# Norm rows and transposed copies of a self-attention layer on ScalarE in place of VectorE

## The chip, the cores and the metric

The kernel runs on one core of a Trainium2 chip. The metric is the device time of one execution in microseconds. The core has five engines that each work through their own instructions in order and wait for each other by semaphores: TensorE (PE in the profile, with its weight loads as PEld), VectorE (DVE), ScalarE (ACT), GpSimd (POOL) and SyncE (SP), which here only issues transfers.

## The reference

Two decoder layers over 32 sequences of 100 tokens with 256 features. Each layer adds self-attention, cross-attention and a mixture of experts to `x`, each applied to the layer norm of `x`:

```python
x = x + _L0_attn_ref(_layernorm(x, axis=-1), ...)
x = x + _L0_xattn_ref(_layernorm(x, axis=-1), ctx_512, ...)
x = x + _L0_ffn_ref(_layernorm(x, axis=-1), ...)
x = x + _L1_attn_ref(_layernorm(x, axis=-1), L1_attn_W1, L1_attn_b1, L1_attn_W2, L1_attn_b2)
x = x + _L1_xattn_ref(_layernorm(x, axis=-1), ctx_512, ...)
x = x + _L1_ffn_ref(_layernorm(x, axis=-1), ...)
```

The layer norm has no learned scale or shift. Layer 1's self-attention has no softmax: the masked scores multiply the values directly.

```python
def _layernorm(x, axis=-1, eps=1e-05):
    m = jnp.mean(x, axis=axis, keepdims=True)
    v = jnp.var(x, axis=axis, keepdims=True)
    return (x - m) / jnp.sqrt(v + eps)

def _L1_attn_ref(x, W1, b1, W2, b2):
    bs, t, d = x.shape
    h = 16
    kqv = x @ W1 + b1
    k, q, v = jnp.split(kqv, 3, axis=-1)
    ...
    mask = jnp.tril(jnp.ones((t, t), dtype=bool))
    attn = jnp.where(mask, jnp.einsum('bhqd,bhkd->bhqk', q, k), 0.0)
    out = jnp.einsum('bhqk,bhkd->bhqd', attn, v)
    out = out.transpose(0, 2, 1, 3).reshape(bs, t, d)
    return out @ W2 + b2
```

## The kernel before

The 3200 tokens lie in SBUF as `x`, 25 tiles of 128 tokens with 256 features. A sequence has 100 tokens, so tiles and sequences don't line up; `parts` and `pieces` say which rows of a tile belong to which sequence. The six parts of the reference run one after the other, each as a loop over sequences, with the norms of the next part made inside the loop of the one before. Everything is float32.

Layer 1's self-attention is `l1_attn`. Before its loop the first tiles are prepared (the fill); then one step per sequence `b` follows. A group is three tiles (the first has four) and serves four sequences. What happens to a tile `f` on its way:

- *Load.* `gather0` (L1356) has SyncE load two rows of layer 0's expert results per token (`yk`, six buffers; the transfer at L1361), and VectorE adds them, weighted, to `x` in two operations (L1368). From the third group on, a load is also tied to an earlier tile's values (`behind`).
- *Stats.* `norm_stats`: mean and variance on VectorE (L219, L222); once a group is complete, one addition (L224), a square root on ScalarE (L225) and a reciprocal on VectorE (L228).
- *Norm row.* `norm_rows` makes `xn` = (x - mean) * rstd, one VectorE operation per tile (L231). Afterwards GpSimd adds the output bias `bo` to `x` (L246).
- *Transposes.* `norm_turn` has TensorE transpose `xn` into a PSUM bank (L253), and `evac` copies the bank to `xnT`. `evac` counts its calls and gives every second to ScalarE (L172), the others to VectorE (L173).
- *Projections.* `proj` makes queries and keys of four sequences (TensorE, L178); ScalarE moves them out with the bias (L1035, L1038). `vals` makes a tile's values; VectorE adds the bias into `vt` (L1048, two operations), and SyncE moves the rows from `vt` to the sequences' `v` (L1055).

In step `b`: the 32 score matmuls (`scores`), into four banks that VectorE empties with the causal mask (L1072, four operations); one projection of the next group; `vals` of a tile in 24 of the steps; `out` of sequence `b - 2` where that completes a tile (L283 adds it to `x`, followed by that tile's stats for the next part); in the first three steps of four, load and stats of a tile of the group after the next; in the fourth, `turn`, that is norm rows and transposes of the next group; and the 32 matmuls of the values of sequence `b - 1` (L1082), copied by ScalarE to `zT` (L1089). `next_norm` prepares norm rows for layer 1's cross-attention on GpSimd (`xnx`); their transposes come a step later, through the same `norm_turn`.

The eight PSUM banks are handed out in turn, so a matmul block also waits for the copy out of what used its bank eight allocations before. TensorE's order is as written (`manual_schedule`). The order on the other engines is chosen by the framework's scheduler from the dependencies. One of these is set by hand: the gather additions come behind `self.last_row`, the norm row that was made last:

```python
self.gather0(pool, fs[i], self.last_row, made[-6] if len(made) > 5 else None)
```

Of the kernel before, what the change touches and what calls it, by code (L numbers as in the profile page):

```python
# [9 lines left out]
F32 = mybir.dt.float32  # L10
I32 = mybir.dt.int32
U32 = mybir.dt.uint32
AF = mybir.ActivationFunctionType
ALU = mybir.AluOpType
AX = mybir.AxisListType

P = 128
# [104 lines left out]
class Kernel:  # L122
# [84 lines left out]
    def norm_stats(self, f, groups, after=None):  # L207
# [15 lines left out]
        if i == n - 1:  # L223
# [3 lines left out]
                self.depend(got, [self.norm_after.ins], "behind the fill's copies")  # L227
            nc.vector.reciprocal(rstd, rstd)  # L228

    def norm_row(self, f, out, eng):  # L230
        return eng.tensor_scalar(out, self.x[:, f, :], *self.norms[f], ALU.subtract, ALU.mult)  # L231

    def norm_rows(self, f, n, bias=None, rows=None, after=None, eng=None):

        nc = self.nc
        if rows is not None:
            xn = rows[:, f : f + n, :]
        else:
            xn = self.lnp.tile([P, 2, XROW], F32, tag="xn", name="xn")[:, :n, :D]
        for j in range(n):  # L240
            got = self.last_row = self.norm_row(f + j, xn[:, j, :], eng or nc.vector)
            if after is not None:
                self.depend(got, [after.ins], "behind the work of its step")
        if bias is not None:
            for j in range(n):
                nc.gpsimd.tensor_tensor(self.x[:, f + j, :], self.x[:, f + j, :], bias, ALU.add)  # L246
        return xn

    def norm_turn(self, f, n, xn, bank):
        pt = bank[:, : NK * n * P].rearrange("p (k c) -> p k c", k=NK)  # L250
        for k in range(NK):
            for j in range(n):
                self.nc.tensor.transpose(  # L253
                    pt[:, k, j * P : (j + 1) * P], xn[:, j, k * P : (k + 1) * P], self.ident,
                )
        self.evac(self.xnT[:, :, f * P : (f + n) * P], pt)

    def xn_at(self, k, f, n=1):

# [723 lines left out]
    def l1_attn(self):  # L983
        nc, tc, a = self.nc, self.tc, self.a
        with ExitStack() as st:
            self.psum = st.enter_context(self.banks("l1a", t=8))
            wk, wq, wv, wo, bqk, bv, bo, xbo = self.w1a
# [14 lines left out]
            bias = cp.tile([P, 3, 2], F32, tag="bias", name="bias")  # L1002
# [9 lines left out]
            q, k, s, later = {}, {}, {}, deque()  # L1012
            self.z_begin(pool, 2)

            def group(i):

                f = (0, 3 * i + 1)[i > 0]
                return range(f, f + FRONT1[f])

            def turn(f, n):  # L1020
                self.norm_turn(f, n, self.norm_rows(f, n, bias=bo), self.bank_m())

            def proj(b0, i):

# [76 lines left out]
            def next_norm():  # L1101
                f = waiting.popleft()
                xn = pool.tile([P, 2, D], F32, tag="xn", name="xnx")
                for j in range(2):
                    self.norm_row(f + j, xn[:, j, :], nc.gpsimd)
                for j in range(2):
                    nc.gpsimd.tensor_tensor(self.x[:, f + j, :], self.x[:, f + j, :], xbo, ALU.add)
                later.append(lambda: self.norm_turn(f, 2, xn, self.bank_m()))

            waiting = deque()  # L1110

# [12 lines left out]
            with tc.manual_schedule(engines={mybir.EngineType.PE}):  # L1124
                for i in range(2):
                    for f in group(i):
                        if i > 0:
                            self.gather0(pool, f, self.last_row)
                            self.norm_stats(f, FRONT1)
                    if i == 0:  # L1130
                        self.norm_after = ahead(AHEAD)
                        for f in group(0):
                            self.norm_stats(f, FRONT1)
                        self.norm_after = None
                    f = group(i)[0]
                    turn(f, 2)
                    turn(f + 2, len(group(i)) - 2)
                    if i == 0:
                        for c in range(4):
                            proj(0, c)  # L1140
                vals(0)
                for b in range(NB + 2):
                    i = b % 4
                    b0 = b - i
                    if b < NB:
                        scores(b)
                    if b0 + 4 < NB:
                        proj(b0 + 4, i)
                    if b in value_at:
                        vals(value_at[b])  # L1150
                    if b > 1:
                        out(b - 2)
                    if b0 + 8 < NB:
                        fs = group(b0 // 4 + 2)
                        if i < 3:
                            self.gather0(pool, fs[i], self.last_row, made[-6] if len(made) > 5 else None)
                            self.norm_stats(fs[i], FRONT1)
                        else:
                            turn(fs[0], 2)
                            turn(fs[2], 1)  # L1160
                    if later:
                        later.popleft()()
                    if waiting:
                        next_norm()
                    if 0 < b <= NB:
                        values(b - 1)
# [1072 lines left out]
```

## Time and profile before

| What | Value |
|---|---|
| median of 3 runs | 2843.68 us (2843.59 to 2845.27) |
| profiled execution | 2870.41 us |
| its span, first to last instruction | 2868.6 us |
| mean granted TensorE clock | 0.984 |
| VectorE waiting for `yk`, 1535 to 1652 us | 1.7 us, once |
| masks L1072, 1530 to 1715 us | 128 operations, 562 ns each |
| gather additions L1368, same stretch | 47 operations, 588 ns each |
| copies of `xnT` on ScalarE, same stretch | 7 of 128x512 (586 ns), 5 of 128x256 (372 ns) |

The profile is of one execution; its times are in microseconds from the first instruction. Busy times of an engine are in microseconds, with the number of instructions in brackets behind an x. In a list in order of time, the columns are start, duration, engine, line, operation, output and inputs, how many in a row, and, in square brackets, the idle time before it with what ended it. In a list of groups, they are line, engine, operation, shapes and count, then busy time, mean duration in nanoseconds, and idle time before with what ended it.

### The profile page before, as it was taken

What the parts mean: (1) busy time and instruction counts of PE and PEld (TensorE: products, weight loads), DVE (VectorE), ACT (ScalarE), POOL (GpSimd) and SP (SyncE); (2) the same over time, 40 slices, a digit from 0 to 9 for tenths busy, and PEclk for the clock granted to TensorE, in tenths of its full rate; (3) what the DMA queues carried; (4) which work ended last, traced back from release to release, by engine and by line L of the source; (5) the groups of instructions that cost most, each with busy time, mean ns of one, the idle gap of its engine ahead of it and who ended that gap; (6) DMA issues with size and microseconds to landing.
All of it is one profiled execution on the core that took longest, in us unless ns stands there. A gap on an engine that the chain in (4) does not pass through costs nothing. (4 is left out here: it accounts for less than half of the span.)

```text
span 2868.6 us, 64252 instructions
## 1 busy us (share of the span) xinstructions
PE 2756.2 (96%) x24856; PEld 2133.5 (74%) x24856; DVE 1773.2 (62%) x5205; ACT 1391.4 (49%) x4210; POOL 765.4 (27%) x960
## 2 busy tenths in 40 slices
PE   8999999999999899999999999999999999999893
PEld 7888888777777656888886777777777777776582
DVE  7666766687888732222226877667676666776453
ACT  5554645677767511222223226556565556567120
POOL 3222212332222243222221230021211302223464
PEclk9999999999999899999999999999999999999997
DMA  7444333000000033665552210010000000000396
GB/s 249 131 134 162 133 141 120 22 16 16 16 16 16 10 124 125 199 210 207 197 201 87 79 42 9 7 50 21 18 15 9 15 9 14 10 11 6 96 269 161
DMA packets 133867, 241.86 MB, mean 84 GB/s; under 512 B 40714, under 2 KB 105925, under 8 KB 126768
## 3 DMA queue, kind: packets, MB, share of 16 engines
q1 hardware_dynamic: 103488, 143.53, 15.9%
q0 software_dynamic: 26784, 90.83, 9.8%
q8 instruction: 200, 3.28, 0.5%
q10 hardware_dynamic: 3280, 3.28, 0.3%
q14 instruction: 115, 0.94, 0.1%
HBM read 152.12 MB, written 111.18 MB: 92 GB/s over the span
## 5 line engine op out<-in xcount | busy, mean ns | idle before, releaser
L1818 POOL DMA_INDIRECT x_d<-xr,slot x200 | 194.9, 975 | 670.4 <-ACT eT L844 591.0
L178 PE MATMUL ps_t<-xnT,wA 128*128 128x200 f32 (+1 forms) x1608 | 321.9, 347 | 1.6 <-DMA wA<-in_wq 1.0
L178 PE MATMUL ps_t<-cT,q 128*128 128x361 f32 (+1 forms) x832 | 307.3, 472 | 0.0
L844 ACT COPY eT<-ps_t 124x384 f32<-124x384 f32 x400 | 191.2, 486 | 225.1 <-PE ps_t L843 219.6
L178 PEld LDWEIGHTS ps_t<-xnT,wA 128*128 128x128 f32 x1608 | 272.5, 191 | 30.1 <-issue 14.5
L834 ACT ACTIVATE wBx<-ps_t,m 128x361 f32<-128x361 f32 x400 | 227.4, 569 | 119.6 <-DVE m L831 109.2
L178 PE MATMUL ps_t<-xT,w 128*128 128x256 f32 (+1 forms) x1276 | 260.2, 363 | 0.7 <-ACT xT L172 0.7
L590 DVE TENSOR_REDUCE m<-ps_t 100x1 f32<-100x361 f32 x512 | 239.7, 524 | 19.3 <-PE ps_t L178 19.1
L178 PEld LDWEIGHTS ps_t<-xT,w 128*128 128x128 f32 x1276 | 223.6, 190 | 36.2 <-issue 9.3
L831 DVE TENSOR_REDUCE m<-ps_t 128x1 f32<-128x361 f32 x400 | 210.6, 527 | 60.3 <-PE ps_t L178 56.9
L843 PEld LDWEIGHTS ps_t<-ident,wBx 128*124 128x124 f32 x1200 | 150.2, 139 | 117.7 <-issue 70.7
L612 ACT ACTIVATE e<-ps_t 121x300 f32<-121x300 f32 x512 | 173.9, 426 | 123.1 <-PE ps_t L178 123.1
L384 ACT ACTIVATE e<-s,m 100x100 f32<-100x100 f32 x512 | 185.6, 364 | 66.2 <-DVE m L378 66.1
L843 PE MATMUL ps_t<-ident,wBx 128*124 128x128 f32 x1200 | 196.8, 275 | 3.6 <-DVE top L1758 2.3
L388 POOL TENSOR_TENSOR e<-e,rz 100x400 f32<-100x400 f32 x128 | 109.3, 855 | 323.7 <-PE ps_t L178 195.4
L178 PE MATMUL ps_t<-wA,cT 128*124 128x512 f32 x384 | 194.5, 594 | 0.0
L1465 DVE TENSOR_TENSOR h<-ps_t,g 128x256 f32<-128x256 f32 (+1 forms) x145 | 58.1, 402 | 188.6 <-ACT g L1464 178.8
L836 DVE TENSOR_SCALAR wBx<-wBx,sums 128x361 f32<-128x361 f32 x400 | 165.6, 414 | 9.4
L178 PEld LDWEIGHTS ps_t<-q,k 32*121 32x121 f32 x3072 | 129.0, 182 | 33.5 <-issue 7.1
L855 PEld LDWEIGHTS ps_t<-eT,v 124*64 124x64 f32 x3072 | 134.9, 137 | 15.2 <-issue 8.1
L1464 ACT ACTIVATE g<-ps_t 128x256 f32<-128x256 f32 (+1 forms) x145 | 52.8, 365 | 191.0 <-PE ps_t L178 165.9
L835 DVE RECIPROCAL sums<-sums 128x1 f32<-128x1 f32 x400 | 63.7, 159 | 126.0 <-ACT wBx L834 123.6
(335 smaller groups left out, 5500.9 us busy)
## 6 DMA issues: line engine op xcount, KB each, us to landing
x_d<-fill SPq DMA_DIRECT2D x16, 1284.0 KB
we<-in_wexp SPq DMA_DIRECT2D x32, 384.0 KB
cT<-in_ctxT SPq DMA_DIRECT2D x64, 186.0 KB
xe_d<-zero SPq DMA_DIRECT2D x8, 1028.0 KB
xe<-x_d SPq DMA_DIRECT2D x24, 321.0 KB
sum<-fill SPq DMA_DIRECT2D x10, 640.0 KB
yk<-y_d SPq DMA_DIRECT2D x25, 256.0 KB
xe<-xe_d SPq DMA_DIRECT2D x24, 257.0 KB
```

The costliest lines, as they stand in the source:

```text
L178: self.nc.tensor.matmul(out, lhsT=l, rhs=r, start=(i == 0), stop=(i == n - 1))
L384: nc.scalar.activation(t[:, i, :], s[:, i, :], AF.Exp, bias=m[:, i : i + 1], accum_out=rz[:, i : i + 1])
L388: nc.gpsimd.tensor_tensor(t[:, h, :], t[:, h, :], self.last(rz[:, h], T), ALU.mult)
L590: got = nc.vector.tensor_reduce(m[:, j, o : o + 1], ps[r], AX.X, ALU.max, negate=True)
L612: nc.scalar.activation(t[:, r], ps[r].rearrange("p (c t) -> p c t", c=NKC), AF.Exp)
L831: self.after = nc.vector.tensor_reduce(m, ps, AX.X, ALU.max, negate=True)
L834: nc.scalar.activation(t, ps, AF.Exp, bias=m, accum_out=z)
L836: nc.vector.tensor_scalar(t, t, z, None, ALU.mult)
L843: nc.tensor.transpose(pt[:, c, :], es[n % 5][:, c * KC : (c + 1) * KC], self.ident)
L844: self.after = nc.scalar.copy(eT[:, :, o : o + P], pt)
L855: nc.tensor.matmul(pz[64 * j : 64 * j + 64, i, :], lhsT=v[:, c, h * 64 : (h + 1) * 64], rhs=eT[:, c, o : o + T], start=(c == 0), stop=(c = ...
L1818: got = nc.gpsimd.indirect_dma_start(out=self.x1_d[:, :], out_offset=bass.IndirectOffsetOnAxis(ap=slot[:, j, k : k + 1], axis=0), in_=xr[: ...
```

## The change

The norm rows of layer 1's self-attention are made by ScalarE: with `shift` = -mean * rstd, a column that VectorE makes, (x - mean) * rstd is x * rstd + `shift`, which is one activation with the function Identity, scale `rstd` and bias `shift`. The dependency of the gather additions is moved from the last norm row to the last `shift`. The copies of `xnT` in this stage, those of the cross-attention's norm rows among them, all go to ScalarE: `act_of` is 1 there in place of 2. `evac` still counts each call, so who copies elsewhere is unchanged. All other calls of `norm_rows` and `norm_turn` do what they did.

```diff
+    def norm_row_act(self, f, out):
+
+        nc = self.nc
+        mean, rstd = self.norms[f]
+        shift = self.lnp.tile([P, 1], F32, tag="shift", name="shift", bufs=4)
+        self.last_shift = nc.vector.scalar_tensor_tensor(shift, mean, -1.0, rstd, ALU.mult, ALU.mult)
+        return nc.scalar.activation(out, self.x[:, f, :], AF.Identity, bias=shift, scale=rstd)
+
     def norm_row(self, f, out, eng):
+        if eng is self.nc.scalar:
+            return self.norm_row_act(f, out)
         return eng.tensor_scalar(out, self.x[:, f, :], *self.norms[f], ALU.subtract, ALU.mult)
 
@@ norm_rows
         for j in range(n):
             got = self.last_row = self.norm_row(f + j, xn[:, j, :], eng or nc.vector)
+            if eng is nc.scalar:
+                self.last_row = self.last_shift
             if after is not None:
                 self.depend(got, [after.ins], "behind the work of its step")
 
-    def norm_turn(self, f, n, xn, bank):
+    def norm_turn(self, f, n, xn, bank, act_of=2):
...
-        self.evac(self.xnT[:, :, f * P : (f + n) * P], pt)
+        self.evac(self.xnT[:, :, f * P : (f + n) * P], pt, act_of)
 
@@ l1_attn
             def turn(f, n):
-                self.norm_turn(f, n, self.norm_rows(f, n, bias=bo), self.bank_m())
+                self.norm_turn(f, n, self.norm_rows(f, n, bias=bo, eng=nc.scalar), self.bank_m(), 1)
...
-                later.append(lambda: self.norm_turn(f, 2, xn, self.bank_m()))
+                later.append(lambda: self.norm_turn(f, 2, xn, self.bank_m(), 1))
```

## The prediction

> **What bounds the kernel now.** I read the page's busy times first, to see which engine could be the bound.
>
> ```profile
> PE 2756.2 (96%) x24856; PEld 2133.5 (74%) x24856; DVE 1773.2 (62%) x5205; ACT 1391.4 (49%) x4210; POOL 765.4 (27%) x960
> ```
>
> TensorE is busy almost throughout, so a VectorE saving is worth only what TensorE loses by waiting for VectorE. The change touches layer 1's self-attention alone, which the chain of waits places at about 1536 to 1714 us. The second view is busy time by stretch there: the fill, the first ten of 32 batch steps, the next ten, the rest.
>
> ```profile
> core 0: us, PE busy (x) PEld busy (x) DVE busy (x) ACT busy (x) POOL busy (x), PEclk, DMA share, GB/s
> 1536.00:1550.00 14.00, 11.88 (x73) 7.09 (x72) 12.93 (x33) 7.25 (x15) 5.59 (x7) 1.00 0.08 19
> 1550.00:1604.00 54.00, 52.18 (x716) 36.83 (x714) 49.64 (x134) 13.74 (x37) 7.41 (x9) 0.97 0.28 80
> 1604.00:1651.00 47.00, 45.89 (x637) 33.47 (x640) 42.39 (x114) 14.01 (x35) 19.55 (x21) 1.00 0.26 74
> 1651.00:1714.00 63.00, 61.20 (x1050) 45.94 (x1049) 47.26 (x116) 16.27 (x45) 22.51 (x28) 1.00 0.15 44
> ```
>
> VectorE is busy 92% and 90% of the middle stretches, ScalarE 25% and 30%. TensorE looks full, but busy time hides waits between matmuls of one block. So third, TensorE's order of time; the 32 score matmuls of a step are one line:
>
> ```profile
> 1591.48 0.96 PE L178 MATMUL ps_t<-qT,kT 32*100 32x100 f32 x32
> ...
> 1595.61 2.38 PE L178 MATMUL ps_t<-qT,kT 32*100 32x100 f32 x32
> ...
> 1602.00 2.05 PE L178 MATMUL ps_t<-qT,kT 32*100 32x100 f32 x32
> ...
> 1681.40 0.96 PE L178 MATMUL ps_t<-qT,kT 32*100 32x100 f32 x32
> ```
>
> 0.96 is the unhindered block; 2.38 and 2.05 contain a wait for PSUM banks that the masking (L1072, VectorE) has not emptied. Excesses over 0.96, steps 1 to 21: 0.96, 2.55 (0.94 of it shown as idle), 1.02, 1.09, 1.42, 1.09, 1.42, 0.29, 0.92, 0.34, 0.13: together **11.2 us**. From step 22 on there is none. After the worst (step 2), one projection took 3.00 instead of 1.61 in the half-clock stretch that shows as 0.97: 1.4 us more. So 12.6 us is all that a faster VectorE could return here.
>
> VectorE's order of time shows what makes it late, a burst every fourth step:
>
> ```profile
> 1591.90 1.11 DVE L231 TENSOR_SCALAR xn<-x_sb,mv,rstd 128x256 f32<-128x256 f32 x2
> 1593.05 2.49 DVE L1368 SCALAR_TENSOR_TENSOR x_sb<-yk,wA,x_sb 128x256 f32<-128x256 f32 x4
> 1595.46 2.00 DVE L1072 TENSOR_TENSOR s<-ps_t,keepT 100x400 f32<-100x400 f32 x4
> ```
>
> Norm rows, then four gather additions that waited for the last row, then the masks TensorE needs. And one place shows another limit: a gather whose rows had not landed (order of time of VectorE, then of the SyncE queue).
>
> ```profile
> 1576.12 0.46 DVE L1048 TENSOR_TENSOR vt<-ps_t,wB 128x128 f32<-128x128 f32 x2
> ...
> 1581.35 1.00 DVE L1368 SCALAR_TENSOR_TENSOR x_sb<-yk,wA,x_sb 128x256 f32<-128x256 f32 x2 [1.73 <-DMA yk<-y_d]
> ```
>
> ```profile
> 1576.61 1.67 SPq L1055 DMA_DIRECT2D v<-vt  x2
> 1578.33 0.47 SPq L1361 DMA_DIRECT2D yk<-y_d  x1
> ```
>
> SyncE issues the moves of a tile's values when `vt` is written (1576.58), and behind them, in order, the load of the tile eleven further on. It landed 4.77 us after the values were written, and VectorE stood still meanwhile.
>
> **The change, part by part.** *Removed from VectorE:* 25 rows and 13 transposed copies. Over 1530 to 1715 us the groups sum to 13.7 us (25 rows, mean 591 ns) and 7.5 + 0.8 us (11 copies of 685 ns, 2 of 414): 22.0 us. *Added to VectorE:* 25 `shift` of one column; the 128x3 operation of L224 takes 163 ns alone, about 70 ns of issue in a series: 1.8 to 4.1 us, taken as 2.5. VectorE falls from 152 to about 133 of 178 us. GpSimd's 25 additions of `bo` (825 ns each, L246) now wait for ScalarE's rows; nothing waits for them before the same tile's out addition, several steps on, so they cost nothing; if the row were a step late, that addition would be next.
>
> *Added to ScalarE:* the nearest row is the query bias, same function and same two column operands:
>
> ```profile
> L1038 ACT ACTIVATE qT<-ps_t,bias,own 128x400 f32<-128x400 f32 x32 | 20.1, 679 | 25.8 <-PE ps_t L178 25.8
> ```
>
> The copies `zT` (L1089) go from 168 ns at 8 columns to 325 at 200, 0.82 ns a column, so 256 columns take 679 - 144 x 0.82 = 561 ns, and 0.46 us in a series (two of L1038 take 1.26, so 0.58 a piece at 400). 25 x 0.46 + 11 x 0.59 + 2 x 0.37 = 18.7 us more on 51.3 of 178: ScalarE stays idle 60% of the stage and hides it, save in the fill. Without that cover the rows would cost 11.5 us.
>
> The Trainium skill ("ScalarE: Activation LUTs", Rules for kernel authors) says to put additions and multiplications on VectorE, not ScalarE; it speaks against this edit. The row of a lone norm row on VectorE, 0.41 us against the 0.56 above, agrees, but by the rule the stage would lose 25 x 0.15 = 3.8 us, and by the stretches, where ScalarE has the room, nothing.
>
> *The fill.* In the built order, ScalarE makes the first four rows behind its last four `v` copies, which end at 1538.49 (VectorE began at 1536.80). Four rows: 3 x 0.46 + 0.56, to 1540.4; both transposed copies follow on the one engine, 2 x 0.59, to 1541.6. The first projection starts at 1541.7 instead of 1540.62: **+1.1**. Until the first scores nothing wins it back (1549.0 against 1547.68). The first `vt`, which before stood behind VectorE's copy and stats, ends at 1549.75 against 1549.85.
>
> *What the gathers wait for next.* They are tied to the last `shift`, no longer to the last row, and the built order puts each pair directly behind the next step's masks, two a step: the burst is gone. SyncE's order is the same instruction for instruction: load 11+j goes out behind the moves of `vt` j, and VectorE's next `vt` now stands behind (or between) that gather's two halves. Waiting with it on VectorE's queue are that `vt`, the stats and the next masks, and TensorE waits for the masks. So a loop closes: `vt` -> moves -> load -> gather -> `vt`. Price of the landing: 4.77 above (seen); the DMA activity by slices lets the load behind the first `vt` end 2.5 us after its issue, 4.4 in all, and a gather never seen waiting gives only "not more than", so 4.2 below. I take 4.55, and 5.15 where three moves stand before it (2.27 of issue, not 1.67). Loop: 4.55 + 0.93 (pair) + 0.42 = 5.9; 5.4 where `vt` stands between the halves. Across a step without values the loop also holds addition, stats of two tiles and masks: 5.15 + 0.45 + 0.42 + 0.45 + 1.1 + 1.95 + 0.4 = 9.9, and with a square root 10.75. From `vt` 1 to `vt` 8: 5.4 + 5.9 + 9.9 + 3 x 5.9 + 10.75 = **49.65**. Before, the same two ends stand at 1554.2 and 1603.4: 49.2. The first `vt` pair starts 1.0 late (1549.75 + 4.55 + 0.45 + 0.42 = 1555.2), so step 9 is 1.5 us late. Carried on with the same pieces through the last seven loads (waits of 0.5 to 1.7 us each), the masks of step 12 come at 1618.3 (before 1618.27), of 16 at 1639.5 (1639.20), of 18 at 1649.1 (1647.73). From step 19 TensorE is the bound in both, and the relief is worth nothing.
>
> **Sum:** +1.3 us: what VectorE sheds it spends standing before its own loads. The profiled execution took 2870.41 us, span 2868.6, so 1.8 outside; the shown runs' median is 2843.68, 26.7 less, and a shift of this stage carries over unscaled: 2843.68 + 1.3 = **2845**. With 4.2 or 4.8 for the landing, some ten closings move by 0.3 each: 2842 to 2848.
>
> **Rivals.** *B, TensorE becomes the bound:* if loads land before VectorE comes to them (under 3.6 us: TensorE's step, 4.98 from the values block at 1665.83 to that at 1670.81, less 0.93 and 0.42), the 12.6 us come back less the fill's 1.1: 2843.68 - 11.5 = 2832; the clock half-step might stay, 2833.6. For it: VectorE's own work would be about 4.85 us a step (1.95 masks, 0.93 pair, 0.45 `vt`, 0.42 addition, 1.1 stats of two tiles), under 4.98. Against: 4.77 was seen. *C, slower:* the same loop, dearer. It decides from 5.5 us a step, the pace of steps 0 to 9 before (1551.53 to 1601.06). If the loads, all now close behind the moves, land like those behind three moves, with the seen 3.00 us of flight (5.35), ten closings cost 0.8 more each: 1.3 + 8 = +9.3, 2853. For it: in the built order each move also waits for an earlier transfer, and some for a free `v` buffer. Against: the slices of DMA activity show the traffic of the loads behind two moves ending 2.4 to 2.8 us after their issue, not 3.0. That the change misses its aim is no rival: the built order has all 25 rows and every copy of the stage on ScalarE.
>
> **How the numbers follow.** Forecast 0.52, B 0.17, C 0.31. What a measurement here can tell is 0.2%, 5.7 us: 2838.0 to 2849.4. The forecast lies within it, B below, C above. The likeliest one's range is 2840 to 2849; the whole, 2835 to 2854, leaves out about half of B and a third of C.
>
> **What would show it.** Waits of VectorE's gather for `yk` rising from 1.7 us (1535 to 1652) to above 10; VectorE's busy time there falling by some 15 with the same length; the first projection near 1 us later after the square root; score blocks still above 0.96 in steps 1 to 18. Wrong if those blocks are at 0.96 and the gather's waits stay few (B), or if `vt` to `vt` takes over 6 us a step (C).

## The result, and the profile after

The changed kernel takes 2857.11 us (median of 6 runs, 2851.37 to 2860.98) beside 2844.47 us for the kernel before (2842.60 to 2846.11): a ratio of 1.0042, 95% interval 1.0032 to 1.0052, so 9 to 15 us slower. Repeated later: 2858.62 beside 2845.82 us, ratio 1.0046 (1.0033 to 1.0060). The forecast was 2845 with a range to 2854; the result lies outside it, on the side of rival C.

The profiled execution after took 2856.18 us (span 2854.5), that of before 2870.41. Before's surplus lies in other stages, so the stages are compared, cut at marks in TensorE's order of time. *Fill*: from the first transposed weight of the stage to the first score matmul. *Steps*: from there to the first score matmul of step 31. The rest, 20.60 us, is the same in all.

| Kernel | fill, us | steps, us | VectorE waiting for `yk` in the steps | VectorE busy around the steps |
|---|---|---|---|---|
| before | 25.25 | 158.90 | 1.7 us, once | 136.2 us |
| after | 25.71 | 168.51 | 23.2 us, 13 times | 118.2 us |

So VectorE has 18 us less to do and the steps take 9.6 us more. Busy time by stretch, after (columns as before; the fill, the steps up to the second of the two long waits shown below, the next 54 us, the rest):

```profile
core 0: us, PE busy (x) PEld busy (x) DVE busy (x) ACT busy (x) POOL busy (x), PEclk, DMA share, GB/s
1522.00:1536.00 14.00, 11.02 (x40) 5.98 (x38) 11.44 (x39) 11.48 (x23) 5.76 (x7) 1.00 0.16 52
1536.00:1590.00 54.00, 44.54 (x601) 31.36 (x600) 35.67 (x106) 17.19 (x42) 6.36 (x9) 0.88 0.24 70
1590.00:1644.00 54.00, 52.13 (x743) 37.20 (x746) 40.67 (x120) 19.72 (x50) 16.18 (x18) 0.96 0.26 75
1644.00:1705.00 61.00, 60.19 (x998) 45.32 (x1002) 41.87 (x108) 20.89 (x53) 24.80 (x27) 1.00 0.15 42
```

In the second stretch VectorE is busy 66% of the time (before 92%) and TensorE 82% (before 97%), at a granted clock of 0.88 (before 0.97): both wait for something else. The waits of VectorE, then of TensorE, in 1524 to 1710 us (who waited for whom, us in total, times, longest):

```profile
DVE x_sb L1380 <- DMA yk<-y_d: 23.2, 13, 3.7
```

```profile
PE ps_t L178 <- DVE vt L1060: 5.9, 5, 3.6
PE ps_t L178 <- DVE x_sb L295: 3.7, 1, 3.7
```

L1380 is the gather addition (L1368 before), L1060 the `vt` addition, L295 the out addition, L1067 the values' moves, L1373 the load. The order of time at the two places where TensorE stood longest:

```profile
1555.44 0.48 DVE L1060 TENSOR_TENSOR vt<-ps_t,wB 128x128 f32<-128x128 f32 x2
...
1555.95 2.27 SPq L1067 DMA_DIRECT2D v<-vt  x3
...
1558.27 0.51 SPq L1373 DMA_DIRECT2D yk<-y_d  x1
1562.13 0.48 DVE L1380 SCALAR_TENSOR_TENSOR x_sb<-yk,wA,x_sb 128x256 f32<-128x256 f32 x1 [3.75 <-DMA yk<-y_d]
1562.53 0.42 DVE L295 TENSOR_TENSOR x_sb<-ps_t,x_sb 128x256 f32<-128x256 f32 x1
...
1563.09 3.00 PE L178 MATMUL ps_t<-xnT,wB 128*128 128x400 f32 x4 [3.71 <-DVE x_sb L295]
...
1586.61 1.33 DVE L1380 SCALAR_TENSOR_TENSOR x_sb<-yk,wA,x_sb 128x256 f32<-128x256 f32 x2 [2.36 <-DMA yk<-y_d]
1587.86 0.48 DVE L1060 TENSOR_TENSOR vt<-ps_t,wB 128x128 f32<-128x128 f32 x2
...
1588.48 1.62 PE L178 MATMUL ps_t<-qT,kT 32*100 32x100 f32 x26 [3.60 <-DVE vt L1060]
...
1590.04 3.03 PE L178 MATMUL ps_t<-xnT,wB 128*128 128x400 f32 x4
```

`vt` is written, its rows are moved, the load goes out behind the moves, and VectorE has already come to that load's gather: it stands 3.75 us. Behind the gather on VectorE's queue is the out addition, which must empty the PSUM bank that TensorE wants next; so TensorE stands 3.71 us. The projection after it takes 3.00 us instead of 1.61. At 1586 the same, with `vt` as the addition that is queued behind. The granted clock was half for 6.8 us from 1560.4 and for 6.8 us from 1587.7.

The Trainium skill ("TensorE: Matmul & The Clock Gate", Part 1: The HAM clock gate) says that TensorE falls to half rate after at least one idle window of about 3.4 us. The trace agrees only in part. Each stretch of 6.8 us goes with a wait of about that length (3.71 and 3.60 us), but it begins inside the wait, 1.0 and 2.8 us after TensorE had stopped, so before 3.4 us of idle time had passed. A third stretch, 3.4 us from 1546.8, follows waits of 0.49 and 1.05 us only. So the rule doesn't account for the moments at which the clock fell here.

### The profile page after: what moved, and what is told of

It is laid out like the page before. It is cut to its first block, busy times and chain, and to the rows that moved or that the text cites. A ratio compares the mean times of both kernels' runs of the same rounds, so it can differ in the third digit from the quotient of the medians.

```text
span 2854.5 us, 64274 instructions
## 1 busy us (share of the span) xinstructions
PE 2749.2 (96%) x24856; PEld 2130.2 (75%) x24856; DVE 1755.2 (61%) x5192; ACT 1408.5 (49%) x4248; POOL 763.7 (27%) x960
## 5 line engine op out<-in xcount | busy, mean ns | idle before, releaser
L178 PEld LDWEIGHTS ps_t<-xnT,wA 128*128 128x128 f32 x1608 | 273.1, 191 | 29.9 <-issue 14.3
```

Of the source, the lines that this page charges most:

```text
L178: self.nc.tensor.matmul(out, lhsT=l, rhs=r, start=(i == 0), stop=(i == n - 1))
```

## The experiments

Two theories stand in the first expectations. *L*: the gathers were put forward (tied to `shift` and not to the row) and have outrun their own loads. *Q*: rows or copies come late on ScalarE. Changes of time are against the kernel before in the same set of runs, by the interval of the ratio; the fill, the steps and the waits are from one profiled execution each (before: 25.25, 158.90 and 1.7 us).

| Run | time less before, us | fill, us | steps, us | waits for `yk`, us |
|---|---|---|---|---|
| changed kernel (first, repeated) | +9 to +15, +9 to +17 | 25.7, 25.5 | 168.51, 169.62 | 23.2, 24.3 |
| e1 gathers behind ScalarE's row | +5 to +10 | 29.9 | 160.38 | 1.6 |
| e2 gathers ahead, ScalarE unchanged | +9 to +17 | 24.6 | 170.34 | 13.1 |
| e3 copies on ScalarE alone | -3 to +2 | 27.8 | 156.94 | 4.0 |
| e4 changed, loads three steps earlier | +1 to +7 | 28.3 | 158.79 | 0 |
| e5 before, loads three steps earlier | -2 to +4 | 24.6 | 160.54 | 0 |
| e6 e4, eight `shift` buffers | +6 to +12 | 25.2 | 163.89 | 8.2 |
| e7 e6, fill on VectorE | +2 to +8 | 25.6 | 159.67 | 5.9 |
| e8 e2, loads three steps earlier | +5 to +11 | 24.8 | 166.63 | 6.7 |
| e9 changed, gathers held, step b - 3 | -14 to -6 | 26.6 | 144.64 | 0 |
| e10 e9, eight buffers, fill on VectorE | -16 to -8 | 25.8 | 144.64 | 0 |
| e11 before, gathers held, b - 3 | -12 to -5 | 25.5 | 150.57 | 0 |
| e12 e9, eight buffers | -13 to -6 | 26.5 | 144.66 | 0 |
| e13 changed, gathers held, b - 4 | -14 to -7 | 25.4 | 144.66 | 0 |
| e14 changed, gathers held, b - 5 | -7 to -2 | 27.9 | 149.61 | 8.6 |

In the sets of e9 to e12 the kernel before took 2871.24 us (another chip), in all others 2844 to 2846; so differences are compared, not times.

**Which part of the change costs.** e1 undoes the moved dependency, e2 makes it alone, e3 makes the copies alone.

```diff
 e1, on the changed kernel: norm_rows
             got = self.last_row = self.norm_row(f + j, xn[:, j, :], eng or nc.vector)
-            if eng is nc.scalar:
-                self.last_row = self.last_shift
 e2, on the kernel before: turn (rstd_of holds each tile's reciprocal, L228)
                 self.norm_turn(f, n, self.norm_rows(f, n, bias=bo), self.bank_m())
+                self.last_row = self.rstd_of[f]
 e3, on the kernel before
-        self.evac(self.xnT[:, :, f * P : (f + n) * P], pt)
+        self.evac(self.xnT[:, :, f * P : (f + n) * P], pt, act_of)
```

> The changed kernel with one thing undone: the gather additions are tied to the last norm row again (now ScalarE's), not to the last shift; rows and copies stay on ScalarE. Theory L (VectorE stands before its own loads because the gathers moved forward): VectorE's waits for yk in the 32 steps fall from 23 us to under 5, the half-clock stretches go with them, and with 20 us of work off VectorE the time comes under the kernel before, by 2 to 8 us (ratio 0.997 to 0.999). Rival Q (rows and copies in ScalarE's queue come late): the gathers don't matter, the time stays 8 to 14 us above before (ratio 1.003 to 1.005).

> The kernel before with one thing of the change: the gather additions are tied to the group's reciprocal instead of its last norm row; rows and copies stay on VectorE as before. Theory L: VectorE's waits for yk rise from 1.7 us to 10 or more, score blocks get longer, the time rises by 6 to 18 us (ratio 1.002 to 1.006), since VectorE has the rows to do besides. Rival Q: nothing of ScalarE's has changed, the time stays within 3 us of before.

> The kernel before with the transposed copies of this stage all on ScalarE, rows on VectorE, gathers behind the row as before. Theory L: 8.4 us off VectorE, waits for yk as before (under 5 us), time 0 to 4 us under before. Rival Q: the copies queue behind other work of ScalarE, 2 to 6 us above before.

e2 took 2856.55 us, ratio 1.0044 (1.0030 to 1.0058): with every row and copy still on VectorE, moving the dependency alone gives the whole loss, and the same two half-clock stretches of 6.8 us. Its VectorE waits, in 1524 to 1710 us:

```profile
DVE x_sb L1372 <- DMA yk<-y_d: 13.1, 11, 3.4
```

e3 took 2845.32 us, ratio 0.9998 (0.9989 to 1.0007): the copies on ScalarE cost nothing that shows in the time (-3 to +2 us). e1 took 2852.53 us, ratio 1.0025 (1.0016 to 1.0034), where L expected it under before: a miss. Tied to the row, the gathers no longer outrun their loads, but now VectorE waits for ScalarE (its waits, 1515 to 1660 us):

```profile
DVE x_sb L1378 <- ACT xn L236: 16.0, 6, 3.3
...
DVE x_sb L1378 <- DMA yk<-y_d: 2.8, 2, 1.6
```

So in e1 VectorE does wait for ScalarE's rows. That this wait makes e1's loss isn't shown: in the profile the steps are only 1.5 us longer than before's, the fill is 4.6 us longer (29.89 for 25.25, with two half-clock stretches of 3.4 us where before's has one), and 6.5 of the 16.0 us stand in the fill.

**Loads earlier.** In e4 the load is split from the additions and issued three steps earlier in the program, with eight `yk` buffers in place of six; e5 is the control without the change, e8 does it to e2. In e6 `shift` has eight buffers, and in e7 also the fill stays on VectorE.

```diff
 e4, on the changed kernel: loop of steps (load_y is the first half of gather0)
+                    if i < 3 and (b0 // 4 + 2) * 3 + 1 + i + 3 < NF:
+                        self.load_y(pool, (b0 // 4 + 2) * 3 + 1 + i + 3, made[-6] if len(made) > 5 else None)
...
 e6, on e4
-        shift = self.lnp.tile([P, 1], F32, tag="shift", name="shift", bufs=4)
+        shift = self.lnp.tile([P, 1], F32, tag="shift", name="shift", bufs=8)
```

> The changed kernel with the loads of yk issued three steps earlier and eight buffers in place of six; all else as changed. Theory L: no load is late any more, waits for yk under 3 us, score blocks near 0.96 throughout, no half-clock stretch in the steps: 6 to 12 us under before (ratio 0.996 to 0.998). Rival Q: still 8 to 14 us above before. If the half clock alone were the cause, apart from the loads, it would also stay above.

> Control: the kernel before (rows, copies and the gathers' place unchanged), with only the loads of yk issued three steps earlier and eight buffers for six. Theory L (the loss of the changed kernel is VectorE standing before loads that come too late for gathers put forward): the kernel before has one such wait of 1.7 us, so early loads give little, within 3 us of before. Rival Q (the loss lies in ScalarE's queue): the same, within 3 us. If this run gains 6 us or more, what the early loads gave the changed kernel (8 us) would be a gain of their own and not the undoing of the loss.

> The changed kernel with early loads as in e4, and with eight buffers for shift in place of four, so that VectorE's shift no longer waits for ScalarE's rows (6.9 us in e4). Theory L with that second wait: waits for yk and for xn both under 2 us, the time within 2 us of before (0 to -2 against before, 2 to 5 under e4). Rival Q: the rows and copies on ScalarE cost by their own place in the fill and in TensorE's wait for xn, so it stays 3 us or more over before.

> As e6, and the first group (the fill) makes its rows and copies as before, so that only the rows and copies of the steps are on ScalarE. Theory L: the fill is as long as before (25.3 us), the steps shorter than before's 158.9 by 2 to 8 us, so 2 to 8 us faster than before and the best of all. Rival Q: TensorE waits for xn and xnT at the turns as in e4 and the steps are not under 158.9: no faster than before.

> As e2 (rows and copies on VectorE as before, the gathers tied to their group's reciprocal, 11 us over before), and with the early loads. Theory L: the loss of e2 goes; within 4 us of before, 8 us or more under e2. Rival Q has no ScalarE row here to blame; if the run stays 8 us or more over before, the loss of e2 is not the late loads but where the gathers stand on VectorE.

e4 took 2849.11 us, ratio 1.0013 (1.0004 to 1.0023): most of the loss is gone, and no wait for `yk` is left. But L expected it 6 to 12 us under before: a miss. Its profile shows a fill 3 us longer than before's, with 6.8 us of half clock in it, and two things in the steps. VectorE waits for free `shift` buffers, which ScalarE's rows still read (waits, 1541 to 1700 us):

```profile
DVE shift L236 <- ACT xn L237: 6.9, 8, 1.8
```

And the additions stand in bursts, as in the kernel before: two pairs, then the masks that TensorE needs (VectorE's order of time):

```profile
1562.85 2.52 DVE L1393 SCALAR_TENSOR_TENSOR x_sb<-yk,wA,x_sb 128x256 f32<-128x256 f32 x4
1565.29 2.00 DVE L1085 TENSOR_TENSOR s<-ps_t,keepT 100x400 f32<-100x400 f32 x4
```

Its score blocks exceed 0.96 us by 10.4 us in all, before's by 11.2.

With eight `shift` buffers the first of the two goes, and e6 was expected 2 to 5 us under e4; it took 2853.71 us, ratio 1.0031 (1.0020 to 1.0043): a miss, and instructive. The gathers are tied to the last `shift`. Once `shift` no longer waits, the scheduler moves the gathers forward as well, and they outrun even the earlier loads: in the built order of e4 the pair that adds the 19th tile stands behind the masks of five steps, in e6 behind those of four, and the waits are back (8.2 us). e8 shows the same on the kernel with VectorE's rows: 2854.04 us, ratio 1.0027 (1.0017 to 1.0037), against the 4 us that L allowed. e7 (2850.11 us, 1.0017, 1.0007 to 1.0027) takes off a part at most and misses its 2 to 8 us under before. e5, 2847.74 us, 1.0003 (0.9994 to 1.0013), shows that early loads are worth nothing to the kernel before. The waits come from too short a distance between a load on SyncE's queue and its addition on VectorE's, and early loads don't set it while the tie lets the additions follow.

**Gathers later.** So e9 to e12 leave the loads where they are and hold the additions: the gathers of step b are tied to the last mask of step b - 3.

```diff
 e9, on the changed kernel: scores, loop of steps
-                    nc.vector.tensor_tensor(
+                    masked[b] = nc.vector.tensor_tensor(
...
-                            self.gather0(pool, fs[i], self.last_row, made[-6] if len(made) > 5 else None)
+                            self.gather0(pool, fs[i], masked.get(b - 3, self.last_row), made[-6] if len(made) > 5 else None)
 e11: the same two edits on the kernel before; e12: e9 with the eight shift buffers
 e10, on e12: turn
+                eng = nc.scalar if f >= FRONT1[0] else None
...
```

> The changed kernel with its loads where they were, and each gather of step b tied to the last mask of step b - 3 in place of the last shift: in the built order every pair then stands one to four steps later than in the changed kernel, one pair a step, never two. Theory L (the loss is VectorE standing before loads that gathers put forward have outrun): waits for yk under 3 us in all (23.2 in the changed kernel), no wait of TensorE above 2 us, no half-clock stretch of 6.8 us behind one, and the steps at 147 to 153 us (before: 158.9, of which 11.2 are score blocks standing for masks and 1.4 a half-clocked projection; these come back when VectorE is relieved by 18 us): 6 to 12 us faster than before, 2833 to 2839. Rival Q (the rows and copies late in ScalarE's queue): 0 to 5 us slower than before. Rival S (a gather directly behind the masks delays the work behind it whether it waits or not): score blocks stay at 8 us or more in excess, steps 157 or more, the same as before.

> As e9, with eight shift buffers in place of four and the fill's rows and copies on VectorE as before. Theory L: as e9, the fill 0.3 to 1 us shorter, so level with it or 1 us faster. Rival Q: as e9 less what the fill costs, up to 3 us faster than e9.

> The kernel before (rows and copies on VectorE) with the gathers tied as in e9. Theory L: no waits for yk, the burst of four gathers gone, VectorE still has its 136 us in the steps: score blocks' excess between 3 and 8 us, so 2 to 8 us faster than before, and 2 to 8 us slower than e9: that difference is what ScalarE's rows and copies are worth once the loads are in time. Rival S: within 2 us of before. If it equals e9 within 2 us, the rows and copies on ScalarE are worth nothing even then.

> As e9 with eight shift buffers alone, to tell the fill and the buffers in e10 apart. Theory L: within 1.5 us of e9, since the shifts of a group stand three steps ahead of its rows' use and do not wait; if VectorE waits in e9 for xn (as in e4, 6.9 us), that wait is gone here and the run up to 3 us faster than e9.

e9 is faster than the kernel before: 2860.18 beside 2871.24 us, ratio 0.9965 (0.9951 to 0.9978). Busy time by stretch in e9, from its fill on, columns as above:

```profile
1531.50:1545.50 14.00, 11.81 (x42) 6.25 (x40) 11.27 (x38) 11.82 (x24) 5.75 (x7) 1.00 0.14 45
1545.50:1590.00 44.50, 44.50 (x693) 32.32 (x696) 39.15 (x112) 19.65 (x47) 6.31 (x9) 1.00 0.34 97
1590.00:1640.00 50.00, 49.88 (x776) 37.38 (x773) 43.76 (x126) 20.57 (x51) 24.43 (x27) 1.00 0.26 76
1640.00:1690.00 50.00, 49.64 (x861) 37.37 (x860) 35.49 (x96) 17.92 (x45) 17.12 (x19) 1.00 0.16 46
```

From the first score on TensorE is busy without a break at a clock of 1.00, all 32 score blocks take 0.96 us, and TensorE's only wait in the steps is 0.4 us. That speaks against rival Q, since every row and copy is still on ScalarE, and against rival S of the expectation, which had the score blocks 8 us or more in excess. The additions stand well behind their loads: from the 12th tile to the 19th, 7.6 to 16.4 us after the load's issue, where the changed kernel has 2.8 to 4.45. (The expectation of e13, below, gives 3.4 to 11.2 for e9; there I had paired each load with the addition before its own.) The 16th tile's load, from SyncE's queue, and its pair of additions, 11.5 us later and with no wait:

```profile
1567.49 0.47 SPq L1373 DMA_DIRECT2D yk<-y_d  x1
```

```profile
1578.98 1.01 DVE L1380 SCALAR_TENSOR_TENSOR x_sb<-yk,wA,x_sb 128x256 f32<-128x256 f32 x2
```

e12 (2861.39 us, 0.9967, 0.9955 to 0.9980) and e10 (2858.70 us, 0.9959, 0.9945 to 0.9972) can't be told from it. e11, with the rows on VectorE, gains nearly as much: 2862.27 us, 0.9969 (0.9957 to 0.9981). In the profiled executions e9's steps are 5.9 us shorter than e11's (144.64 against 150.57, where score blocks exceed 0.96 by 4.5 us), but the intervals of the times overlap, so what ScalarE's rows are worth, once the loads are in time, the times don't show; L had put it at 2 to 8 us.

e11 also shows that the hold gains by more than the distance. The kernel before had only 1.7 us of waits for `yk` to lose, and with early loads alone (e5) it gained nothing. But in e11 the pairs stand one a step, where before often has two behind the same masks, and the score blocks' excess falls from 11.2 to 4.5 us. The hold changes both, how far an addition stands behind its load and how the additions are spread, and no run parts the two in e9.

**How the loss depends on the distance.** e13 and e14 hold the gathers by one and two steps less; e15 is the changed kernel on the same chip.

```diff
 e13, on e9
-                            self.gather0(pool, fs[i], masked.get(b - 3, self.last_row), made[-6] if len(made) > 5 else None)
+                            self.gather0(pool, fs[i], masked.get(b - 4, self.last_row), made[-6] if len(made) > 5 else None)
 e14: b - 5
```

> As e9, each gather tied to the masks of step b - 4 in place of b - 3: one step (4 to 5 us) nearer to its load. In e9 the first gather of a run of three starts 3.4 to 11.2 us after its load was issued, and flights of 2.8 to 4.5 us were seen. Theory L, gradual: some loads are now passed by the gather, waits for yk of 2 to 8 us in all, steps of 145 to 152 us, 4 to 10 us faster than before. At once: as e9, no wait, within 1.5 us of it.

> As e9, tied to the masks of step b - 5: in the built order one step behind the changed kernel's place, on the first gather of each three (behind the masks of steps 4, 8, 12 in place of 3, 7, 12), and one pair a step. Theory L, gradual: waits for yk of 8 to 18 us in all, steps of 152 to 164 us, between 4 us faster and 8 us slower than before. At once: as the changed kernel, 8 us or more slower than before, or, if one step of distance is already enough, as e9.

> The changed kernel, for its time on this chip: 9 to 15 us slower than before, as in the first comparison (ratio 1.0032 to 1.0052).

On one chip with the kernel before at 2845.82: the changed kernel 2858.62 us; held at b - 5, 2839.89 (0.9983, 0.9974 to 0.9992); at b - 4, 2835.89 (0.9964, 0.9950 to 0.9977). At b - 5 a pair stands at most one step later than in the changed kernel (the 14th tile's behind the masks of four steps for three, the 17th's of eight for seven, the 20th's at the same place; the expectation counted the steps a little differently), and that turns 13 us of loss into 6 us of gain. VectorE's waits in b - 5 around the steps, then in the changed kernel repeated:

```profile
DVE x_sb L1380 <- DMA yk<-y_d: 8.6, 6, 3.0
```

```profile
DVE x_sb L1380 <- DMA yk<-y_d: 24.3, 13, 3.6
```

15.7 us of waits less make the steps 20.0 us shorter (169.62 to 149.61): more than the waits. In the steps of b - 5 no half-clock stretch is left (the changed kernel has 17.0 us in three), and the score blocks' excess falls from 11.7 to 5.0 us. Neither expectation for e14 fits: it is gradual, as the waits are between those of the changed kernel and of b - 4, but steeper than I had put it (149.6 us against 152 to 164). At b - 4 no load is late any more, and b - 3 brings nothing further, as the second expectation for e13 had it. e13 is 22.7 us under the changed kernel and 9.9 under the kernel before, by medians of one chip. The waits alone don't set the length of the steps, though: e6 has 8.2 us of them and steps of 163.89 us, b - 5 has 8.6 us and 149.61; in e6 most pairs stand two behind the same masks, in b - 5 one a step.

## Why the prediction was wrong, point by point

- *"VectorE falls from 152 to about 133"*: right. Around the steps it fell by 18.0 us (136.2 to 118.2). `shift` took 2.5 us for 25, as taken; ScalarE's rows 13.9 us (613 ns each) against 11.5, hidden.
- *Copies and GpSimd's additions cost nothing*: e3 shows it for the copies. For GpSimd the profile shows no engine waiting for L258.
- *Fill +1.1*: 25.71 against 25.25, +0.5; but before's fill begins with 3.4 us of half clock and after's has none, so the pair isn't clean.
- *"What VectorE sheds it spends standing before its own loads"*: the mechanism is right. e2 shows that the moved dependency alone makes a loss of this size, and with the additions held (e13) it is gone. Waits for `yk` rose from 1.7 to 23.2 us, where I had put "above 10".
- *"I take 4.55, and 5.15 where three moves stand before it"*, with 4.2 to 4.8 as bounds: **this term failed.** From the end of `vt` to the start of the gather, the eight landings from the first `vt` (number 0, ahead of the table below) to the eighth (number 7) took 4.9, 4.5, 5.2, 6.2, 4.8, 6.1, 4.8 and 5.7 us: mean 5.3, where my mixture makes 4.7. The price came from one seen wait of 4.77 and a reading of coarse slices. The loop closes on it each step, so a mean error of 0.57 counts eight times: 4.6 us, of which 4.2 lie in the table.
- *No term for TensorE's stand and the clock behind it.* I let the loop pass through VectorE and SyncE only, and named the half clock for rival B alone. Where the landing was 1.06 us late (3-4 in the table below), TensorE stood for 3.71 us and was granted half the clock, and the next `vt` came later still.

My sum by its own pieces, beside the ends of `vt` in the profile of after (each taken as the start of its first move less 0.03 us):

| from `vt` to `vt` | 1-2 | 2-3 | 3-4 | 4-5 | 5-6 | 6-7 | 7-8 | sum |
|---|---|---|---|---|---|---|---|---|
| predicted, us | 5.4 | 5.9 | 9.9 | 5.9 | 5.9 | 5.9 | 10.75 | 49.65 |
| measured, us | 5.35 | 6.62 | 12.19 | 6.17 | 7.52 | 6.54 | 11.04 | 55.43 |

The two worst are 3-4 (the landing 1.06 over 5.15, then the projection 1.4 longer at half clock) and 5-6 (the landing 1.57 over 4.55). Of the 5.8 us by which the sum is off, the landings make 4.2 and that projection 1.4. With 1.3 us lost before `vt` 1 and 2.1 after `vt` 8, the 6.2 us by which this stretch exceeds before's 49.2 make the 9.6 us of the steps.

- *Rival C* ("the same loop, dearer", 2853) was right in its kind, and by its own sign: `vt` to `vt` over 6 us in four of the five single steps. It priced the flight, from a load's issue to its gather, at the one seen 3.00 us (measured 2.8 to 4.45), and also had no half clock in it.
- *Rival B* ("if loads land before VectorE comes to them", the 12.6 us come back) needed a condition that the change didn't meet. Where e9 and e13 meet it, the steps fall by 14.3 us, 1.7 more than I called the most a faster VectorE could return, and the time by about 10. But the condition alone isn't enough: e4 meets it too, with no wait for `yk`, and its steps stay at 158.8 us with the additions in bursts.
- *"Score blocks still above 0.96 in steps 1 to 18"*: right, with the same sum (11.1 us for 11.2), so it did not tell the forecast from the slower kernel: what was lost went into the waits between the blocks.

The rule that I had weighed against the change, to keep additions and multiplications off ScalarE (the Trainium skill, "ScalarE: Activation LUTs", Rules for kernel authors), does not explain the loss: e2 has it without a row on ScalarE, and e9 gains with all of them there. Still open is why the landings took so different times (more on this in the last section), and what the rows on ScalarE are worth in time once the loads are early enough.

## What to carry to other kernels

When work leaves an engine or a dependency is tied to something earlier, look in the built order at what moves forward into the gap, and measure how far each consumer then stands behind the transfer it needs; early issue alone gave back a part at most here, since the consumers were free to follow or to bunch, so tie each consumer to a step of its own. In a loop that closes through a transfer, price the landing by the spread of several, not by one seen wait, and multiply its uncertainty by the number of closings before writing the range. If TensorE hangs on that loop, add what a halved clock behind its waits costs (here 3.00 us in place of 1.61 for a projection).

## What the runs showed of the hardware

The same load of 256 KB had very different flights. Two stretches of the changed kernel's DMA activity, 1543 to 1549 us and 1573 to 1582 us, each in 40 slices (busy tenths of the DMA engines, then GB/s):

```profile
DMA  0000000000000001876633775456879840000000
GB/s 0 0 0 0 0 0 0 0 0 0 0 0 0 0 0 55 205 177 177 205 123 109 232 205 164 123 130 232 300 266 341 280 144 27 0 0 0 0 0 0
```

```profile
DMA  0000002000003851229487722222211000000000
GB/s 0 0 0 0 0 0 73 0 0 0 0 0 146 228 164 37 55 73 173 168 237 246 173 68 100 82 96 96 86 68 36 0 0 0 0 0 0 0 0 0
```

Both hold two moves and one load, 0.52 MB. In the first the load (issued at 1545.63) runs at up to 341 GB/s and its gather starts 2.8 us after the issue; in the second (issued at 1575.95) the rate sinks below 100 GB/s with the engines two tenths busy, and the gather starts after 4.45 us. The moves issued ahead of the load were slow with it: their packets (2 KB each, the load's 1 KB) end 1.4 us after the load's issue in the first stretch and 3.3 us after it in the second, where single ones took up to 0.84 us against 0.20, and the load's last packet ends 1.0 and 0.7 us behind them. It isn't chance: in the repeated profile of the changed kernel the same two loads reached their gathers after 2.74 and 4.46 us. Why these moves were slow is open.

In this stage half-clock stretches came in lengths of 3.4 and 6.8 us, in every run that has any; the three of the changed kernel begin 13.6 and 27.3 us apart, four and eight times 3.4. The profiled fills of e3, e4 and e14 (27.8, 28.3 and 27.9 us against 25.3 before) each hold one of 6.8 us, that of e1 (29.9 us) two of 3.4 us; whether the fill's length follows from the kernel or changes from run to run, one profile of each doesn't tell.
